# Sums of attention weights added on GpSimd, single banks of logits, and output transposes one step later

## The chip, the cores and the metric

One core of a Trainium2 chip runs one launch of the kernel. The metric is the device time of that launch in microseconds (us). Names of the engines: PE is TensorE (PEld its weight loads), DVE is VectorE, ACT is ScalarE, POOL is GpSimd, SP is SyncE, which issues most of the DMAs. PSUM has eight banks of 128 x 512 float32; a "pair" is two of them.

## The reference

The network has four layers, each an attention-like block and a feed-forward block, added to x (4 x 512 x 512, float32) with gates. The kernel runs them as stages 0 to 7 (`s0` to `s7` in the names). Two stages matter here: stage 0, cross-attention of 16 heads of 32 with 496 keys and 16 more keys of their own projection ("DCA"), and stage 6, cross-attention of 32 heads of 16 with 512 keys.

```python
def _L0_xattn_ref(x, y, Wq, bq, Wk, bk, Wv, bv, Wkv_dca, bkv_dca, ...):
    y_dca = y[:, -DCA:, :]
    y_main = y[:, :-DCA, :]
    kv_dca = (y_dca @ Wkv_dca + bkv_dca).reshape(b, DCA, 2, H, HD)
    k_dca = _ln(kv_dca[:, :, 0], kn_dca_w, kn_dca_b)
    v_dca = kv_dca[:, :, 1]
    q = _ln((x @ Wq + bq).reshape(b, s1, H, HD), qn_w, qn_b)
    ...
    k = _ln(kv[..., :HD], kn_w, kn_b)
    v = kv[..., HD:]
    ctx = _attn(qT, k, v)            # softmax over 496 keys
    ctx_dca = _attn(qT, k_dca, v_dca)
    return (ctx + DCA_WEIGHT * ctx_dca) @ Wo + bo
```

The softmax subtracts each row's maximum, takes the exponential, and divides by the sum of the weights over the keys.

## The kernel before

Products are in float32 unless bf16 is named. Stage 0 works on four batches b, in each on four groups g of four heads, in each on four tiles k of up to 128 keys, and in each tile on two pairs i of heads. One turn of the innermost loop is called a slot here: 32 slots a batch, eight a group. The logits are kept with keys on partitions and queries along the row, so that the weights can go straight into the product with the values.

A slot of stage 0 (`s0`, the loop at the end of the function) does this:

- TensorE: the logits of two heads into a pair of banks `pl` (`together`, the matmul at L262, two products on different rows of the array side by side), and, beside them, two products `ps` for the row maxima of a group to come (12 slots, `LEAD`, ahead). Then the maxima, transposed and split in three bf16 parts (`mT`), are subtracted by a product with ones into the same `pl` banks.
- ScalarE: the exponential of the pair, 128x1024, into a tile `pr` (L757). There is one `pl` buffer, so the next slot's logits wait for it.
- VectorE: the reduction of `ps` to maxima `nmx` (L634).
- TensorE: a four-head product of an earlier tile's `pr`, by the values into bank `av` in one slot of the tile, by ones into bank `sm` in the other (`weigh`; its inner `sums`, L649 and following). Both are added up over the four key tiles in PSUM.

When a group's last tile is in, `av` and `sm` are copied to `o` and `ri` on ScalarE (L671), four reciprocals of 128x128 (L673) and a product (L674) run on VectorE, then `summed` adds the DCA part: one product `pd` (L682), then `oT` (L687). After the last group of a batch, `project` multiplies by the output weights (`po`, L238), adds the bias and the residual (L772).

The next batch's projections, norms and transposes are cut into pieces (`pieces`, `todo`), and one is issued behind a slot at even distance through the first 20 slots of each batch. PSUM in stage 0 is `pl` (2 banks), two pairs `sc` that all other work shares in turn, `av` and `sm`.

The order on TensorE is partly written by hand: a product that is "tied" (`tie`, L244) follows the one tied before it; the rest is placed by the scheduler. `together` ties always, `chain` (L234) when told to.

In stage 6 a slot is alike, with three single banks of logits, two exponentials of 128x512 (L1846), a reduction per bank (L1728), and products by values in two halves of 256 queries, one half a slot. The values carry a column of ones, so the sums come with them. After a group's last half, the bank `av` is copied to `oT` on ScalarE (L1765), and `norm` (L1768) is put in the list `behind`, which is emptied one call at a slot's end: four transposes of `oT` (`s_pt`, by `flip`, L1495), a reciprocal (L1778) and a product (L1779). A piece of other work is issued at a slot's end when `behind` is empty.

Of the kernel before, what the change touches and what calls it, by code (L numbers as in the profile page):

```python
# [19 lines left out]
P = 128  # L20
# [28 lines left out]
class Net:  # L49
# [222 lines left out]
    def s0(self):  # L272
        nc, a = self.nc, self.a
        H, HD, M, ND = 16, 32, 496, 16
        LEAD = 12
        cxs = {0: self.context("s0", 0)}
        wkv = self.w("s0_wkv").rearrange("p (c n) -> p c n", c=CC)
        wq = self.w("s0_wq").rearrange("p (c n) -> p c n", c=DC)
        wd = self.u("s0_wd").rearrange("p (c n) -> p c n", c=CC)
# [16 lines left out]
        nc.sync.dma_start(wd, a["s0_wd"].rearrange("(c p) n -> p c n", p=P))  # L296
# [25 lines left out]

        def weights():
            pn = self.sc("s0_pn")[:, 0, 0:6]
            self.chain(pn, [(rep.rearrange("p r m -> p (r m)"), nw32)], tied=True)
            nc.vector.tensor_copy(nw, pn)
            nc.vector.tensor_scalar(nw[:, 0:2], nw[:, 0:2], HD**-0.5, None, op0=ALU.mult)
# [38 lines left out]
        def pieces(b):  # L366
# [11 lines left out]
            def small(k):  # L378
                room["v" + k] = self.s(f"s0_va{k}_{b}", TB * H, f"s0_va{k}")
                room[k] = self.u(f"s0_{k}4_{b}")  # L380

            def kv(k):
                if k == 0:
                    small("k")
                pkv = self.sc(f"s0_pkv_{b}_{k}")
                for i in range(2):
                    self.chain(
                        pkv[:, i, :],
                        [
                            (cx[:, c, k * P : (k + 1) * P], wkv[:, c, i * 512 : (i + 1) * 512])  # L390
                            for c in range(CC)
                        ],
                        tied=b == 0,
                    )
                dst = room["k"][:, k * 512 : (k + 1) * 512]
                nc.vector.tensor_tensor(dst, pkv[:, 0, :], bk, op=ALU.add)
                nc.scalar.copy(v4[:, k, :], pkv[:, 1, :])
# [4 lines left out]
            def half(k, y):  # L402
# [3 lines left out]
                    heads(room[k][:, y * 1024 : (y + 1) * 1024]),  # L406
# [3 lines left out]
            def turned(k, y, dst, wi):  # L410

                pt = self.sc(f"s0_pt{k}_{b}_{y}").rearrange("p i (g n) -> p i g n", g=4)
                for i in range(2):
                    for g in range(4):
                        lo = (2 * y + i) * 512 + g * P
                        nc.tensor.transpose(pt[:, i, g, :], room[k][:, lo : lo + P], self.ident)
                for i in range(2):
                    lo = (2 * y + i) * P
                    nc.scalar.activation(
                        dst[:, :, lo : lo + P], pt[:, i], AF.Identity,  # L420
                        scale=nw[:, wi : wi + 1], bias=nw[:, wi + 1 : wi + 2],
                    )

            def xT(y):
                if y == 0:
# [8 lines left out]
                    room["xT"] = self.u(f"s0_xT_{b}").rearrange("p (c n) -> p c n", c=DC)  # L434
                pt = self.sc(f"s0_ptx_{b}_{y}")
                for i in range(2):
                    for t in range(TB):
                        nc.tensor.transpose(
                            pt[:, i, t * P : (t + 1) * P],
                            room["xl"][t][:, (2 * y + i) * P : (2 * y + i + 1) * P],  # L440
                            self.ident,
                        )
                self.evict(y, room["xT"][:, 2 * y : 2 * y + 2, :], pt)

            def query(y):
                if y == 0:
                    small("q")
                pq = self.sc(f"s0_pq_{b}_{y}")
                for i in range(2):
# [3 lines left out]
                        [(room["xT"][:, c, t * P : (t + 1) * P], wq[:, c, :]) for c in range(DC)],  # L453
                    )
                nc.vector.tensor_tensor(
                    room["q"][:, y * 1024 : (y + 1) * 1024].rearrange("p (i n) -> p i n", i=2),
# [3 lines left out]
                )  # L460
                for t in (2 * y, 2 * y + 1):
                    squares(
                        f"s0q_{b}_{t}",
                        room["q"][:, t * 512 : (t + 1) * 512],
# [4 lines left out]
            def short():  # L469

                kbd = made["kbd"]
                ps = self.sc(f"s0_ld_{b}").rearrange("p i (t n) -> p (i t) n", n=256)
                for t in range(TB):
                    for g in range(4):
                        nc.tensor.matmul(
                            ps[:, t, 64 * g : 64 * (g + 1)],
                            lhsT=qT[:, g, t * P : (t + 1) * P],
                            rhs=kbd[:, b, g, :],
                            start=True, stop=True,
# [4 lines left out]
                w = self.up.tile([P, TB * H, ND], F32, tag="pr", name=f"s0_ws_{b}", bufs=4)  # L484
                nc.vector.tensor_reduce(mx, v, axis=AX.X, op=ALU.max, negate=True)
                nc.vector.tensor_tensor(w, v, wide(mx), op=ALU.add)
# [6 lines left out]
            def shortT():  # L493
                pt = self.sc(f"s0_ptw_{b}")
                for y in range(2):
                    for t in range(TB):
                        nc.tensor.transpose(
                            pt[:, y, t * P : (t + 1) * P], room["w"][:, t, y, :], self.ident
                        )
                nc.scalar.copy(wT, pt)  # L500
# [20 lines left out]
        def second():  # L521


            centre("wd", wd[:, :, 0:512].rearrange("p c (h d) -> p c h d", d=HD))
            centre("bd", heads(bd))
            pk = self.sc("s0_pkd")[0:NK, 0, :]
            self.chain(
                pk, [(cd[:, c].rearrange("p b k -> p (b k)"), wd[:, c, 0:512]) for c in range(CC)]
# [3 lines left out]
            nc.vector.tensor_tensor(kd, pk, bd[0:NK], op=ALU.add)  # L532
# [4 lines left out]
        def keys():  # L537
            kd = made["kd"]
            pt = self.sc("s0_ptd")[:, 0, 0 : 4 * NK].rearrange("p (g b k) -> p b g k", g=4, b=NB)
            for g in range(4):  # L540
                nc.tensor.transpose(
                    pt[:, :, g, :].rearrange("p b k -> p b k"),
                    kd[:, g * P : (g + 1) * P],
                    self.ident[0:NK, 0:NK],
                )
            kbd = fixed("s0_kbd", [P, NB, 4, 64])
            nc.gpsimd.memset(kbd, 0.0)
            for j in range(4):
                rows = slice(32 * j, 32 * (j + 1))
                nc.vector.tensor_scalar(  # L550
                    kbd[rows, :, :, ND * j : ND * (j + 1)], pt[rows],
                    nw[rows, 4:5], nw[rows, 5:6], op0=ALU.mult, op1=ALU.add,
                )
            cr = self.u("s0_cr")[:, 0 : CC * NB * P].rearrange(
                "p (c b r k) -> p c b r k", c=CC, b=NB, r=8
            )
# [11 lines left out]
            made["kbd"], made["cr"], made["mask"] = kbd, cr, mask  # L568
            made["vbd"] = fixed("s0_vbd", [P, NB, D])
            nc.vector.tensor_tensor(bvs[:, 0, :], bvs[:, 0, :], bvs[:, 1, :], op=ALU.add)  # L570

        def values(b):
            pv = self.sc(f"s0_pvd_{b}")[:, 0, :]
# [3 lines left out]
                    (made["cr"][:, c, b].rearrange("p r k -> p (r k)"), wd[:, c, 512:1024])  # L577
                    for c in range(CC)
                ],
            )  # L580
            nc.vector.tensor_tensor(made["vbd"][:, b, :], pv, made["mask"], op=ALU.mult)

        maxT, lead = {}, []

        def maxima():

            freed = lead

            def turn(b, g, nmx):
# [6 lines left out]
                pt = self.ps2.tile([P, TB * P], BF16, tag="sc", name=f"s0_ptm_{b}_{g}")  # L596
                for t in range(TB):
                    nc.tensor.transpose(
                        pt[:, t * P : (t + 1) * P],
                        m3[:, t].rearrange("p j k -> p (j k)"),  # L600
                        self.ident16,
                    )
                maxT[b, g] = self.vp.tile([P, S], BF16, tag="mT", name=f"s0_mT_{b}_{g}", bufs=3)
                self.evict(g, maxT[b, g], pt)

            waiting = None
            for b in range(NB):
                kT, qT = made[b][0:2]
                for g in range(4):
                    nmx = self.s(f"s0_nmx_{b}_{g}", 16, "s0_nmx")  # L610
                    for t in range(TB):
                        for y in range(2):
# [4 lines left out]
                            name = f"ps_s0_{b}_{g}_{t}_{y}"  # L617
                            if alone[0] and y:
                                ps = self.ps4.tile([P, 2, S], F32, tag="pl", name=name)
                            else:  # L620
                                ps = self.sc(name)
                            parts = []
                            for i in range(2):
                                rows = slice(32 * (2 * y + i), 32 * (2 * y + i + 1))
                                parts.append((
                                    ps[:, i, 0:M],
# [5 lines left out]
                            def after(ps=ps, nmx=nmx, at=4 * t + 2 * y):  # L632
                                with self.tc.high_priority():
                                    i = nc.vector.tensor_reduce(  # L634
                                        nmx[:, at : at + 2], ps[:, :, 0:M],
                                        axis=AX.X, op=ALU.max, negate=True,
                                    )
                                freed.append(i.ins)

                            yield parts, freed[-2:-1], after  # L640
# [3 lines left out]
        behind, later = Behind(), Behind()  # L644
        av, sm, oTs = {}, {}, {}

        def weigh(b, g, k, prs):

            v4 = made[b][2]  # L649
            n = min(P, M - k * P)  # L650
            if k == 0:
                av[g] = self.ps1.tile([P, S], F32, tag="av", name=f"s0_av_{b}_{g}", bufs=1)
                sm[g] = self.ps1.tile([P, S], F32, tag="sm", name=f"s0_sm_{b}_{g}", bufs=1)
            flags = dict(start=(k == 0), stop=(k == TB - 1))

            def part(out, lhs):
                parts = []
                for j in range(4):
                    h = slice((4 * g + j) * HD, (4 * g + j + 1) * HD)
                    parts.append((  # L660
                        out[HD * j : HD * (j + 1), :], lhs(h), prs[j // 2][0:n, j % 2, :], flags
                    ))
                self.together(parts)

            def sums():
                part(sm[g], lambda h: self.ones[0:n, 0:HD])
                if k == TB - 1:

                    o, ri = self.t(f"s0_o_{b}_{g}"), self.t(f"s0_ri_{b}_{g}")
                    nc.scalar.copy(o, av[g])  # L670
                    nc.scalar.copy(ri, sm[g])  # L671
                    for c in range(0, S, P):
                        nc.vector.reciprocal(ri[:, c : c + P], ri[:, c : c + P])  # L673
                    nc.vector.tensor_tensor(ri, ri, o, op=ALU.mult)  # L674
                    behind(summed, b, g, ri, more=True)

            part(av[g], lambda h: v4[0:n, k, h])
            later(sums, more=True)

        def summed(b, g, r):  # L680
            pd = self.sc(f"s0_pd_{b}_{g}")[:, 0, :]
            nc.tensor.matmul(  # L682
# [1373 lines left out]
```

## Time and profile before

| | us |
|---|---|
| median of 3 runs | 3339.56 |
| lowest, highest | 3332.45, 3341.3 |
| profiled execution | 3345.06 |
| its span | 3343.2 |
| mean granted TensorE clock | 0.923 of full |

| engine | busy, us | share of the span |
|---|---|---|
| PE | 2877.5 | 86% |
| PEld | 1440.6 | 43% |
| DVE | 1972.4 | 59% |
| ACT | 1215.7 | 36% |
| POOL | 629.3 | 19% |

The page of the profile gives the busy time of each engine, the span cut in 40 equal slices with the busy share of each in tenths, the chain of work that ended last, and the costliest groups of instructions, each with its line, its tiles, its count, busy time and mean duration, and what ended the idle time before it. Further views of the same trace give a table of stretches of time, the waits of one engine (who waited for whom, in total, how often, the longest), one tile's or one line's instructions, and the instructions in order of time. A line in these views may be that of a helper: all of `together` is L262, all of `chain` L238. The trace has 1.9 us outside its span.

### The profile page before, as it was taken

The page shows a single profiled execution, that of the slowest core. Times are in us where ns is not written, and L with a number is a line of the kernel's source. Part 1 is how long each engine was busy: PE and PEld are TensorE (multiplying, and loading weights), DVE is VectorE, ACT ScalarE, POOL GpSimd, SP SyncE. Part 2 cuts the span into 40 slices and gives each one's busy share as a digit, 9 for nine tenths or more (in the row PEclk, how much of TensorE's full clock was granted, in tenths as well). Part 3 has the DMA queues.
Part 4 walks back from the last instruction along what each step waited for, and adds up shares of the span by engine and source line. Part 5 has one row for each costly group of instructions (what it writes and reads, how often), then busy time and mean ns, then how long its engine had stood idle before and what let it go on. Part 6 is the DMA issues. An engine that isn't in the chain of part 4 may idle for free.

```text
span 3343.2 us, 42023 instructions
## 1 busy us (share of the span) xinstructions
PE 2877.5 (86%) x15644; PEld 1440.6 (43%) x15648; DVE 1972.4 (59%) x3148; ACT 1215.7 (36%) x1948; POOL 629.3 (19%) x509
## 2 busy tenths in 40 slices
PE   7999889959888989998845699978899999889994
PEld 3333233224444444444423588852333333254673
DVE  7555556468898979875678311138666666634103
ACT  2343433355554444432322111113544444520231
POOL 0000000006564655750000122210000000000351
PEclk8989999969899989999977699988999999989997
DMA  4000000058676777861222599972000000022798
GB/s 127 7 1 7 1 1 9 1 210 232 188 231 181 228 205 223 242 181 57 80 74 74 181 323 323 324 268 69 14 27 14 27 1 1 1 76 79 260 384 315
DMA packets 266617, 438.67 MB, mean 131 GB/s; under 512 B 32384, under 2 KB 114560, under 8 KB 264880
## 3 DMA queue, kind: packets, MB, share of 16 engines
q1 hardware_dynamic: 250352, 386.72, 36.5%
q0 software_dynamic: 13760, 45.10, 3.7%
q10 hardware_dynamic: 2304, 4.20, 0.3%
q8 instruction: 124, 2.03, 0.3%
q14 instruction: 77, 0.63, 0.1%
HBM read 370.79 MB, written 65.13 MB: 130 GB/s over the span
## 4 chain that ended last, share of the span: by engine, by line
PE 37%; DVE 7%; ACT 4%; issue 3%; POOL 2%; DMA 2%; POOLq 0%; DVEq 0%; ACTq 0%
PE s_po L238 8%; PE s_pl L262 8%; PE pg_s L238 6%; ACT pr_s L1846 3%; PE s_ph L238 2%; PE s_pq L238 2%; PE s_av L262 1%; DVE x L772 1%; DMA s_y<-s_ys 1%; PE s_pr L238 1%; PE s_pkv L238 1%; PE pt_s L217 1%; POOL s_ys L1364 1%; PE s_pb L238 1%; DVE st_s L174 1%
## 5 line engine op out<-in xcount | busy, mean ns | idle before, releaser
L1055 POOL TENSOR_TENSOR s_h<-s_h,s_C 128x512 f32<-128x512 f32 x256 | 447.6, 1749 | 302.8 <-DVE s_h L1054 264.4
L1846 ACT ACTIVATE pr_s<-s_pl 128x512 f32<-128x512 f32 x512 | 277.9, 595 | 339.2 <-PE s_ps L262 324.9
L1728 DVE TENSOR_REDUCE s_top<-s_ps 128x1 f32<-128x512 f32 x512 | 328.5, 685 | 110.6 <-PE s_ps L262 110.4
L1054 DVE TENSOR_TENSOR_SCAN s_h<-s_da,s_db 128x512 f32<-128x512 f32 x256 | 312.0, 1219 | 66.9 <-PE s_y L262 39.7
L262 PE MATMUL s_pl<-s_qT,s_kT 32*128 32x512 f32 x1024 | 293.5, 649 | 29.2 <-ACT pr_s L1846 5.7
L1053 ACT ACTIVATE s_da<-s_rdl,s_A 128x512 f32<-128x512 f32 x256 | 184.4, 722 | 336.6 <-DVE s_h L1054 334.5
L262 PE MATMUL s_ps<-s_kT,s_qT 32*128 32x512 f32 x1024 | 291.4, 661 | 7.8 <-DVE s_top L1728 5.8
L238 PE MATMUL s_ph<-xT_s,s_wu 128*128 128x256 f32 x1024 | 251.9, 402 | 0.7 <-ACT xT_s L161 0.7
L814 PE MATMUL s_acc<-s_wd,s_hT 128*128 128x512 f32 x512 | 239.9, 612 | 7.0 <-ACT s_hT L845 7.0
L262 PE MATMUL s_av<-pr_s,s_v 128*32 128x256 f32 (+2 forms) x2560 | 237.8, 443 | 0.2
L238 PEld LDWEIGHTS s_ph<-xT_s,s_wu 128*128 128x128 f32 x1024 | 200.9, 201 | 79.5 <-issue 48.2
L238 PEld LDWEIGHTS pg_s<-s_xbT,s_w 128*128 128x128 f32 (+1 forms) x1872 | 214.2, 184 | 19.8 <-issue 17.8
L634 DVE TENSOR_REDUCE s_nmx<-ps_s 128x2 f32<-128x992 f32 x128 | 151.2, 1184 | 117.3 <-PE ps_s L262 117.3
L238 PE MATMUL pg_s<-s_xbT,s_w 128*128 128x128 f32 (+1 forms) x1872 | 215.8, 276 | 1.4 <-ACT s_xbT L161 1.4
L1052 DVE TENSOR_TENSOR s_db<-s_B,s_rdu 128x512 f32<-128x512 f32 x256 | 202.7, 792 | 13.6 <-DMA s_B<-s_bc 5.9
L757 ACT ACTIVATE pr_s<-pl_s 128x1024 f32<-128x1024 f32 (+1 forms) x128 | 131.0, 1024 | 194.0 <-PE pl_s L262 164.8
L262 PE MATMUL s_y<-s_h,ident 64*64 64x512 f32 x1024 | 148.5, 643 | 52.1 <-issue 33.4
L1443 DVE TENSOR_TENSOR g_s<-g_s,pg_s 128x256 f32<-128x256 f32 x78 | 27.5, 353 | 263.7 <-ACT g_s L1442 263.7
L262 PE MATMUL pl_s<-s_qT,s_kT 32*128 32x512 f32 (+1 forms) x512 | 154.2, 680 | 26.1 <-ACT pr_s L757 23.0
L262 PE MATMUL ps_s<-s_kT,s_qT 32*128 32x496 f32 x512 | 153.5, 713 | 8.7 <-DVE s_nmx L634 7.5
L814 PEld LDWEIGHTS s_acc<-s_wd,s_hT 128*128 128x128 f32 x512 | 93.4, 192 | 152.1 <-issue 115.9
L1337 POOL DMA_INDIRECT s_xb<-s_xs,s_from x86 | 83.2, 967 | 379.8 <-PE ptr_s_xb L228 228.8
(375 smaller groups left out, 4282.7 us busy)
## 6 DMA issues: line engine op xcount, KB each, us to landing
s_B<-s_bc SPq DMA_DIRECT2D x256, 256.0 KB
s_C<-s_bc SPq DMA_DIRECT2D x256, 256.0 KB
s_w<-in_s_wg SPq DMA_DIRECT2D x39, 704.0 KB
s_w<-in_s_wu SPq DMA_DIRECT2D x39, 704.0 KB
s_w_rt<-in_s_ru SPq DMA_DIRECT2D x47, 512.0 KB
s_w_rt<-in_s_rd SPq DMA_DIRECT2D x47, 512.0 KB
s_w<-in_s_wd SPq DMA_DIRECT2D x39, 512.0 KB
s_y<-s_ys SPq DMA_DIRECT2D x32, 512.0 KB
```

What stands on the lines that cost most here:

```text
L238: ins = self.nc.tensor.matmul(out, lhsT=l, rhs=r, start=(i == 0), stop=(i == len(pairs) - 1)).ins
L262: ins = self.nc.tensor.matmul(out, lhsT=l, rhs=r, **flags).ins
L634: i = nc.vector.tensor_reduce(nmx[:, at : at + 2], ps[:, :, 0:M], axis=AX.X, op=ALU.max, negate=True,)
L757: nc.scalar.activation(prs[i][0:n], pl[0:n], AF.Exp)
L814: ins = nc.tensor.matmul(accs[i][t], lhsT=hT[:, j, t * P : (t + 1) * P], rhs=wd[f // 4][:, f % 4, :], start=(f == 0), stop=(f == FC - 1),).ins
L1052: nc.vector.tensor_tensor(db, br, du, op=ALU.mult)
L1053: nc.scalar.activation(da, dl, AF.Exp, scale=am[:, e, n : n + 1])
L1054: nc.vector.tensor_tensor_scan(h, da, db, 0.0, op0=ALU.mult, op1=ALU.add)
L1055: nc.gpsimd.tensor_tensor(h, h, cr, op=ALU.mult)
L1337: self.nc.gpsimd.indirect_dma_start(out=t, out_offset=None, in_=self.sorted[name][1], in_offset=bass.IndirectOffsetOnAxis(ap=fr[:, j : j + ...
L1728: ins = nc.vector.tensor_reduce(dst[:, i], ps[i][0], axis=AX.X, op=ALU.max, negate=True).ins
L1846: ins = nc.scalar.activation(prs[i][:, j, :], pl[j][0], AF.Exp).ins
```

## The change

In stage 0:

- The weights are added up over the four key tiles on GpSimd: for each pair of heads of a group, three additions of 128x1024, the first into a tile `es` of its own (`added`). One four-head product by ones a group then takes the place of four (`sums`), one slot after the last product by values. The bank `sm` is gone; the product goes to a pair of `sc`, as do `pd`, `po` and all other work, through one function (`dealt`).
- The product by values is made in two halves of 256 queries, one half in each of two slots.
- The logits have three single banks instead of one pair, with two exponentials of 128x512 instead of one of 128x1024. The products of a slot wait for the readers of the banks that they need (`before`).
- All products and transposes of the main loop are tied, in the order of the program. The two halves of `project` are a slot apart (`soon`), and the remaining pieces of two kinds are mixed.
- Evictions of `mT`, and of `xT` from the second batch on, are all on ScalarE. The tiles of 2048 columns are parted in two of 1024, `s0_wd` in two tiles with a DMA each, and the spread DCA keys `kbd` are made for each batch by four small copies on GpSimd. In the lead, half of the maxima's reductions are one bank each.

In stage 6 an empty entry is put into `behind` ahead of `norm`, so that the transposes come a step later.

```diff
-        wd = self.u("s0_wd").rearrange("p (c n) -> p c n", c=CC)
+        wds = [
+            self.up.tile([P, CC, 512], F32, tag="pr", name="s0_wd0", bufs=PR),
+            ut("s0_wd1").rearrange("p (c n) -> p c n", c=CC),
+        ]
...
+        sets = {"sc": 2, "pl": 3}
+        readers = {tag: [] for tag in sets}
+
+        def dealt(name, tag="sc"):
+
+            if tag == "sc":
+                t = self.sc(f"s0_{name}")
+            else:
+                t = self.ps4.tile([P, S], F32, tag=tag, name=f"s0_{name}")
+            readers[tag].append([])
+            return t, readers[tag][-1].append
+
+        def before(tag, n):
+
+            old = readers[tag][-n - sets[tag] - 1 : -sets[tag]]
+            return [r[-1] for r in old if r]
...
+        def spread(b):
+            for j in range(4):
+                rows = slice(32 * j, 32 * (j + 1))
+                nc.gpsimd.tensor_copy(
+                    kbd[b % 2][rows, :, ND * j : ND * (j + 1)], made["kc"][rows, b]
+                )
...
-                self.evict(g, maxT[b, g], pt)
+                maxT[b, g] = self.vp.tile([P, S], BF16, tag="mT", name=f"s0_mT_{b}_{g}", bufs=2)
+                read(nc.scalar.copy(maxT[b, g], pt).ins)
...
-        def weigh(b, g, k, prs):
+        def weigh(b, g, k, prs, half):
...
+            cols = slice(half * (S // 2), (half + 1) * (S // 2))
...
+                    prs[j // 2][0:n, j % 2, cols],
...
+                o = self.t(f"s0_o_{b}_{g}")
+                nc.scalar.copy(o, av[g])
+                soon(1, sums, b, g, o)
+
+        def added(b, g, k, i, pr):
+
+            n = min(P, M - k * P)
             if k == 0:
+                es[i] = pr
+                return
+            to = es[i]
+            if k == 1:
+                to = self.up.tile([P, 2, S], F32, tag="es", name=f"es_s0_{b}_{g}_{i}", bufs=ES)
+            nc.gpsimd.tensor_tensor(to[0:n], es[i][0:n], pr[0:n], op=ALU.add)
+            es[i] = to
...
-            def sums():
-                part(sm[g], lambda h: self.ones[0:n, 0:HD])
-                if k == TB - 1:
...
-            part(av[g], lambda h: v4[0:n, k, h])
-            later(sums, more=True)
+        def sums(b, g, o):
+
+            sm, read = dealt(f"sm_{b}_{g}")
+            sm = sm[:, 0, :]
+            self.together([
+                (
+                    sm[HD * j : HD * (j + 1), :], self.ones[:, 0:HD],
+                    es[b, g, j // 2][:, j % 2, :], dict(start=True, stop=True),
+                )
+                for j in range(4)
+            ])
+            ri = self.t(f"s0_ri_{b}_{g}")
+            read(nc.scalar.copy(ri, sm).ins)
+            for c in range(0, S, P):
+                nc.vector.reciprocal(ri[:, c : c + P], ri[:, c : c + P])
+            nc.vector.tensor_tensor(ri, ri, o, op=ALU.mult)
+            soon(2, summed, b, g, ri)
...
-                    behind(project, b, y, more=True)
+                    soon(2 + y, project, b, y)
...
-                        pl = self.ps4.tile([P, 2, S], F32, tag="pl", name=f"pl_s0_{b}_{g}_{k}_{i}")
+                        pl = [dealt(f"pl_{b}_{g}_{k}_{i}_{j}", "pl") for j in range(2)]
...
-                        nc.scalar.activation(prs[i][0:n], pl[0:n], AF.Exp)
+                        for j in range(2):
+                            ins = nc.scalar.activation(prs[i][0:n, j, :], pl[j][0][0:n, :], AF.Exp).ins
+                            pl[j][1](ins)
                         if after:
                             after()
-                        flush((later, behind)[i])
-                        if i == 1:
-                            behind(weigh, b, g, k, prs, more=True)
+                        added(b, g, k, i, prs[i])
+                        if i == 0:
+                            for half in range(2):
+                                soon(1 + half, weigh, b, g, k, prs, half)
+                        flush()
...
@@ stage 6 @@
                 nc.scalar.copy(oT, avs[g])
+
+                behind(lambda: None, more=True)
                 behind(norm, b, g, oT, more=True)
...
-        gp=1, cp=1, wp=3, kq=2, vp=2, up=3, bp=3, tp=6, sp=2, ps4=1, ps2=2, ps1=1
+        gp=1, cp=1, wp=3, kq=2, vp=2, up=5, bp=3, tp=5, sp=2, ps4=3, ps2=2, ps1=1
```

## The prediction

> **What bounds the kernel now.** Stage 0 takes the first 692 us and stage 6 runs from 2255 to 2958 (read from the windows of the trace); nothing else is touched. I read the page's slices first.
>
> ```profile
> PE   7999889959888989998845699978899999889994
> ...
> POOL 0000000006564655750000122210000000000351
> ...
> PEclk8989999969899989999977699988999999989997
> ```
>
> A slice is 83.6 us, so stage 0 is the first eight digits and stage 6 the 28th to 35th. In both TensorE is at 8 or 9 tenths after the first slice; in stage 0 GpSimd is idle and the granted clock 0.8 to 0.9 or so. So TensorE's own work and short waits set the time. The groups of stage 0 and their counts, by shape (window 77 to 692):
>
> ```profile
> L634 DVE TENSOR_REDUCE s_nmx<-ps_s 128x2 f32<-128x992 f32 x117 | 138.5, 1184 | 112.2 <-PE ps_s L262 112.2
> ...
> L757 ACT ACTIVATE pr_s<-pl_s 128x1024 f32<-128x1024 f32 x96 | 98.3, 1024 | 149.4 <-PE pl_s L262 126.2 <-PE ps_s L262 22.4 <-PE s_sm L262 0.5
> ...
> L673 DVE RECIPROCAL s_ri<-s_ri 128x128 f32<-128x128 f32 x64 | 54.2, 909 | 39.1 <-ACT s_ri L671 38.8
> ```
>
> The timeline then shows one slot of stage 0 (start, duration, engine, what; a block of products overlaps itself):
>
> ```profile
> 391.42 0.70 PE L262 MATMUL pl_s<-s_qT,s_kT 32*128 32x512 f32 x2 [0.17 <-ACT pr_s L757]
> ...
> 392.38 0.38 PE L262 MATMUL pl_s<-s_mT,s_ones 32*128 32x512 bf16 x2
> ...
> 392.86 1.02 ACT L757 ACTIVATE pr_s<-pl_s 128x1024 f32<-128x1024 f32 x1 [1.50 <-PE pl_s L262]
> 393.94 0.19 PEld L262 LDWEIGHTS pl_s<-s_qT,s_kT 32*128 32x128 f32 x2 [1.09 <-ACT pr_s L757]
> ...
> 395.21 1.06 PE L262 MATMUL s_sm<-pr_s,ones 128*32 128x512 f32 x8
> ...
> 396.21 0.40 PE L598 MATMUL s_ptm<-ident,s_split 128*128 128x128 bf16 x4
> ```
>
> A plain slot lasts 393.94 - 391.42 = 2.52 us: logits and maxima 0.96, the subtraction of the maxima 0.31, one block by values or by ones 1.00 (395.21 to 396.21), and a wait of about 0.2 for the exponential, which holds the only pair of logits banks. All such waits in 77 to 692 sum to 23.0 us in 41 times. A group of four heads is eight slots. In stage 6 TensorE's waits (total, times, longest) are led by one:
>
> ```profile
> PE s_pt L1495 <- ACT s_oT L1765: 30.4, 29, 1.1
> ```
>
> The output transposes stand right behind the last product by values and wait for the copy of its bank.
>
> **Sum products.** 64 blocks by ones become 16: 48 x 1.00 = **48 us** of TensorE work gone. That is the gain only where TensorE is the limit.
>
> **Plain slots.** Afterwards a slot has 0.96 + 0.31 + half a block by values. Half of 1.00 plus 0.05 gives 1.82. But the exponential begins 1.38 to 1.44 after the slot's first logits, the first half frees a bank after 0.595 (the 128x512 exponential of stage 6, L1846), and the next logits follow 0.06 later: 1.38 + 0.595 + 0.06 = 2.04. The exponential, not TensorE, then limits such a slot: gain 0.48, not 0.70. Two halves cost ScalarE 1.19 instead of 1.02, inside 2.04.
>
> **Groups with nothing beside them.** Before, the first reciprocals (L673) of such neighbours stand 22.36 us apart (545.06 to 567.42, and 603.57 to 625.93). VectorE's work per group: eight reductions x 1.19, four reciprocals 3.4, the product 0.67, the output 0.75, splits about 1.1, in all 15.4. The reciprocals are one burst, and a product that needs a bank pair waits behind it. I followed the new order slot by slot from the one that holds the sum product, at 0: sum product 1.82 to 2.85, copy to 3.5, reciprocals to 7.0, the waiting reduction to 8.2. The pair products of the DCA values (`pd`) are now dealt into the same rotation of two pairs and are tied, so they wait from 6.2 to 8.2; the next maxima wait another 1.35 behind the product. Six other slots take 2.04, and the next sum product's slot begins at 21.8. Gain **0.57 a group**: the burst takes back nearly all of 8 x 0.48 - 1.00.
>
> **Groups with pieces of the next batch beside them.** TensorE is full there. In 20 of 32 slots a batch, 0.50 goes and 1.00 per group comes back: 20 x 0.50 - 2.5 = 7.5. The remaining twelve give between nothing and 0.47 each; with the rows above I take 8 to 9.7 a batch, together some **38 us** in stage 0. Batch 3's last twelve slots have no maxima and keep 0.45 each; they are in that sum.
>
> **GpSimd's additions.** Six of 128x1024 a group. The nearest row is stage 4's addition of half the size (its source's durations, ns: least 1265, median 1772, most 3504; 128x512, two operands in SBUF, VectorE busy beside it). Doubled: 2.53 to 7.0 us, and 3.5 by the mean of 1749. I take 2.5 to 3.5, since stage 0's VectorE mostly reads PSUM while stage 4's multiplies and scans SBUF tiles all the time. In the order above the sum product wants the last addition at 23.6; the additions become ready at 2.6, 5.4, 7.5, 13.8, 16.2 and 18.2. At 2.53 the last ends at 21.3, hidden; at 3.5 at 24.3, 0.6 late. From 3.3 on they show, and at 5 the group is GpSimd's, 30 us.
>
> The row also says that the two engines disturb each other: the stage 4 product on VectorE (L1052) has a least time of 686, a mean of 792 and a most of 1771 ns. The product behind the reciprocals (L674) reads two SBUF tiles while additions run; a wait of up to one addition there delays a reduction and so TensorE. I charge 3 to 8 us for stage 0.
>
> [...]
>
> **Other edits of stage 0.** The sums after the last group wait for the last addition and their copy: +2 us, at the end, uncovered. In the lead, six pair reductions become twice as many single-bank ones, about +1. The eight-product output block (L238, `po`) is parted and moved one slot; eleven evictions move from VectorE (L162, 0.42 for the maxima) to ScalarE; an exponential may wait behind one, 0 to 5 us in all: I take 0, since most fall in slots where TensorE is full. The waits behind table loads (up to 3.9 us of `pl` on ScalarE, some four places) stay. SP: the loads for the next stages wait now for the last group's addition and weights, still ahead of the last output, so ctx, which comes last, is not later; if that cover failed, their issue (506 to 514 us before) costs up to 8.
>
> **Clock.** In 10-us windows of stage 0 the granted clock falls to 0.50 to 0.76 where TensorE waited some 2 us or more; over the stretches at 0.87 to 0.94 the missing share of the clock times their length comes to some 44 us of stage 0. New waits of 2.05 and 1.35 us close together could bring more such windows (2 to 3.5 us each), and fewer waits elsewhere fewer: ±10, taken as 0.
>
> Stage 0: -38 + 2 + 1 + (3 to 8, say 3) = **-32 us**.
>
> **Stage 6.** A slot with the transposes lasts 3.36 (2420.39 to 2423.75), its neighbours 1.81 (2427.43 to 2429.23).
>
> ```profile
> 2422.52 0.59 ACT L1765 COPY s_oT<-s_av 128x512 f32<-128x512 f32 x1
> ...
> 2423.16 0.66 PE L1495 MATMUL s_pt<-ident,s_oT 128*128 128x128 f32 x4 [1.06 <-ACT s_oT L1765]
> ```
>
> One step later the four transposes still cost 0.60, but by then the copy, which ends 2.7 to 2.95 after that slot's start, is done before TensorE reaches them, at 3.6 or later. The 1.06 goes. What is late next is the exponential chain: 5.7 us in 28 times already, of which a part may go too. The queue behind the transposes is the next slot's logits, as before; reciprocal and product come a slot later on VectorE, which is 1.29 busy in 1.81 and has room for 0.68. Bounds 25 to 35; I take the row, 30.4, and 1 more: **-31**.
>
> **Sum.** -32 - 31 = -63 against the profiled execution: 3345.1 (span 3343.2) to 3282. That execution lies 5.5 above the median of the runs, 3339.6; from there the forecast is **3276**.
>
> **Rivals.**
> 1. *All of the sum products' time comes out* (0.17): the burst is hidden, the exponential chain shortens with the pairs gone, half of the 23.0 of waits go. -48 - 11, stage 6 -33: 3340 - 92 = 3248. For it: TensorE 8 to 9 tenths busy. Against: 2.04 by the exponential's row.
> 2. *Only one stage gives* (0.20): stage 0's gain is eaten by the burst, the additions' disturbance of VectorE and a colder clock, stage 6 keeps its 31: 3309; or the reverse, the exponential takes the place of the copy in stage 6 and stage 0 keeps 32: 3308. For it: 0.57 a group against 48 us of work removed.
> 3. *GpSimd becomes the bound and the kernel is slower* (0.08): at 5.3 us an addition a group takes 32 us of GpSimd, and the sum product waits for it. The eight intervals between first reciprocals that were 20.3 to 33.6 before (210 in sum) and some 1.8 less after are stretched to 32: 256 - 210 + 14 = 60 lost, the point from which there is no gain. At 6 us, 36 a group, it is 32 more and 2 of the next interval: 94, so 3276 + 94 = 3370. For it: the 3504 row, doubled. Against: the median, doubled, is 3.5.
> 4. *Little moves* (0.05): the ties and the additions at about 5 us just balance stage 6: 3335.
>
> The forecast has 0.50. The range 3243 to 3318 takes in the first two rivals and leaves out the last two, 0.13. Faster by over 0.3% (10 us, about what a measurement here can tell from none): 0.50 + 0.17 + 0.20 = 0.87; within 0.05; slower 0.08.
>
> **What would show it.** In the profile after: first reciprocals of bare groups 21 to 22.5 us apart; plain slots of about 2.04; additions of 128x1024 between 2.5 and 3.5 us; `pd` waiting for VectorE some 2 us in bare groups; the wait for L1765 gone and stage 6 some 31 us shorter; stage 0 ending at about 660. Additions of over 4 us, or a wait of the sum product for GpSimd in most groups, would make it wrong.

## The result and the profile after

| | before | after |
|---|---|---|
| median of the runs, us | 3341.16 (12 runs) | 3342.31 (12 runs) |
| span of the profiled execution, us | 3343.2 | 3344.0 |
| stage 0, to the next stage's first product (`s_pi`), us | 691.1 | 722.4 |
| TensorE idle in stage 0, from 80 us on, us | 59.1 | 113.9 |
| time lost to a lower granted clock there, us | 43.8 | 74.0 |
| stage 6, first input transpose to last output product, us | 710.7 | 681.3 |

The ratio of after to before is 1.0003, 95% interval 0.9993 to 1.0013: no change that can be measured, where 63 us less were forecast. The two stages went opposite ways: stage 6 gave 29 us and stage 0 took 31. The fourth row is the sum over stretches of 4 us of the time in which TensorE is not busy, the fifth that of their length times the missing share of the clock; where TensorE waits at a low clock both count it, 5.4 us of before and 7.9 of after. What is left of stage 0 from 80 us on, about TensorE's work at full clock, went from 509 to 456 us. So the 48 us of sum products did go, with 3 to 5 more; 55 us of waiting and 30 us of low clock came in their place.

The rows of the page of after that were shown of before:

```profile
PE   6888887877998998998855699995999999989994
...
POOL 0333334424565554770000022210000000000351
...
PEclk8889998778998998999976699996999999989997
```

GpSimd is busy for some three tenths of the first eight slices; TensorE has lost about a tenth there, and in the eighth slice the clock has fallen to 7. TensorE's waits in the first 720 us (total, times, longest):

```profile
PE s_pl L262 <- ACT pr_s L859: 28.9, 30, 4.2
PE s_pd L238 <- DVE s_nmx L693: 20.7, 10, 3.2
PE s_pl L262 <- DVE s_nmx L693: 16.7, 7, 4.0
...
PE s_sm L262 <- POOL es_s L750: 2.0, 1, 2.0
```

The sum product waits for GpSimd once, at the end. The waits that grew are for VectorE's reductions (L693; L634 before), since before these were:

```profile
PE ps_s L262 <- DVE s_nmx L634: 7.5, 9, 1.4
...
PE s_pd L682 <- DVE s_nmx L634: 1.8, 2, 0.9
...
PE pl_s L262 <- DVE s_nmx L634: 0.8, 1, 0.8
```

In stage 6 the wait for the copy is gone (of 30.4 before):

```profile
PE s_pt L1599 <- ACT s_oT L1869: 0.7, 1, 0.7
```

Why VectorE is late shows in the durations of its instructions that have both operands in SBUF, the on-chip memory beside PSUM, or cast one from there (least, median, most in ns; line by line, before first: the casts and the differences that split the maxima, and the product behind the reciprocals):

```profile
L593 DVE CAST s_split<-s_nmx x48: 190/203/205, 70.1 to 633.9; 128x16 bf16<-128x16 f32 x48
...
L595 DVE TENSOR_TENSOR s_nmx<-s_nmx,s_split x32: 111/185/189, 70.4 to 633.6; 128x16 f32<-128x16 f32 x32
...
L674 DVE TENSOR_TENSOR s_ri<-s_ri,s_o x16: 674/676/692, 139.1 to 674.8; 128x512 f32<-128x512 f32 x16
```

```profile
L647 DVE CAST s_split<-s_nmx x48: 135/203/2355, 75.9 to 657.1; 128x16 bf16<-128x16 f32 x48
...
L649 DVE TENSOR_TENSOR s_nmx<-s_nmx,s_split x32: 183/185/2327, 76.1 to 656.9; 128x16 f32<-128x16 f32 x32
...
L750 POOL TENSOR_TENSOR es_s<-es_s,pr_s x64: 2337/2347/3172, 103.2 to 697.8; 128x1024 f32<-128x1024 f32 x32, 112x1024 f32<-112x1024 f32 x32
...
L770 DVE TENSOR_TENSOR s_ri<-s_ri,s_o x16: 675/1400/2626, 143.0 to 705.8; 128x512 f32<-128x512 f32 x16
```

The medians of casts and differences are as before, but their most is the length of one addition (15 of the 80 lasted longer than before, counted in the trace); the product's median itself has doubled. One group's burst in the timeline of after:

```profile
587.58 2.34 POOL L750 TENSOR_TENSOR es_s<-es_s,pr_s 128x1024 f32<-128x1024 f32 x1 [1.26 <-ACT pr_s L859]
587.69 2.29 DVE L647 CAST s_split<-s_nmx 128x16 bf16<-128x16 f32 x1
589.87 1.18 DVE L693 TENSOR_REDUCE s_nmx<-s_ps 128x2 f32<-128x992 f32 x1
590.97 0.73 DVE L780 SCALAR_TENSOR_TENSOR s_oT<-s_pd,s_bvs,s_ri 128x512 f32<-128x512 f32 x1
...
591.19 1.22 PE L262 MATMUL s_pl<-s_qT,s_kT 32*128 32x512 f32 x2 [4.03 <-DVE s_nmx L693]
```

A cast of 128x16, 0.2 us of work, starts 0.11 after an addition and ends when the addition does (at 589.98; 587.58 + 2.34 = 589.92). The reduction queued behind it ends 2.1 us late. The logits are issued together with the product for the next maxima, which needs that reduction; they wait 4.03, of which the cast made 2.1. When TensorE goes on it is slow: the pair takes 1.22 instead of 0.70.

### The profile page after: what moved, and what is told of

It is laid out like the page before. It is cut to its first block, busy times and chain, and to the rows that moved or that the text cites. A ratio compares the mean times of both kernels' runs of the same rounds, so it can differ in the third digit from the quotient of the medians.

```text
span 3344.0 us, 42659 instructions
## 1 busy us (share of the span) xinstructions
PE 2854.8 (85%) x15772; PEld 1448.2 (43%) x15776; DVE 2000.9 (60%) x3140; ACT 1229.3 (37%) x2087; POOL 859.4 (26%) x622
## 4 chain that ended last, share of the span: by engine, by line
PE 37%; DVE 7%; ACT 3%; issue 3%; DMA 2%; POOL 2%; SPq 0%; POOLq 0%; DVEq 0%; ACTq 0%
PE s_po L238 8%; PE s_pl L262 8%; PE pg_s L238 6%; ACT pr_s L1952 2%; PE s_ph L238 2%; PE s_pq L238 2%; PE s_av L262 2%; DMA s_y<-s_ys 1%; DVE x L876 1%; PE s_pkv L238 1%; PE s_pr L238 1%; PE pt_s L217 1%; POOL s_ys L1468 1%; PE s_pb L238 1%; POOL s_xb L1441 1%
## 5 line engine op out<-in xcount | busy, mean ns | idle before, releaser
L262 PE MATMUL s_pl<-s_qT,s_kT 32*128 32x512 f32 (+1 forms) x1536 | 462.4, 679 | 78.8 <-ACT pr_s L859 28.9
L262 PE MATMUL s_ps<-s_kT,s_qT 32*128 32x512 f32 (+1 forms) x1536 | 450.7, 689 | 13.9 <-DVE s_top L1832 5.9
L262 PE MATMUL s_av<-pr_s,s_v 128*32 128x256 f32 (+1 forms) x3072 | 258.9, 410 | 0.2
L262 PEld LDWEIGHTS s_pl<-s_qT,s_kT 32*128 32x128 f32 (+1 forms) x1536 | 121.9, 192 | 248.8 <-ACT pr_s L1952 95.9
L859 ACT ACTIVATE pr_s<-s_pl 128x512 f32<-128x512 f32 (+1 forms) x256 | 138.8, 595 | 200.4 <-PE s_pl L262 167.9
L693 DVE TENSOR_REDUCE s_nmx<-s_ps 128x2 f32<-128x992 f32 x122 | 144.4, 1184 | 94.2 <-PE s_ps L262 94.2
L750 POOL TENSOR_TENSOR es_s<-es_s,pr_s 128x1024 f32<-128x1024 f32 (+1 forms) x64 | 152.9, 2395 | 170.6 <-ACT pr_s L859 170.2
L262 PEld LDWEIGHTS s_av<-pr_s,s_v 128*32 128x32 f32 (+1 forms) x3072 | 62.2, 110 | 297.6 <-issue 265.5
```

Source lines behind the costliest of these rows:

```text
L262: ins = self.nc.tensor.matmul(out, lhsT=l, rhs=r, **flags).ins
L693: ins = nc.vector.tensor_reduce(nmx[:, at : at + 2], pair[:, :, 0:M], axis=AX.X, op=ALU.max, negate=True,).ins
L750: nc.gpsimd.tensor_tensor(to[0:n], es[i][0:n], pr[0:n], op=ALU.add)
L859: ins = nc.scalar.activation(prs[i][0:n, j, :], pl[j][0][0:n, :], AF.Exp).ins
```

## The experiments

Theory A: the additions delay VectorE, instruction by instruction, and through the reductions behind them TensorE. Theory B: the burst of reciprocals and the tied order stop TensorE by themselves. Ratios below are to runs of the kernel before on the same chip, with 95% intervals; times are medians.

**Stage 6 alone.** The kernel before with one line more.

```diff
                 nc.scalar.copy(oT, avs[g])
+                behind(lambda: None, more=True)
                 behind(norm, b, g, oT, more=True)
```

> The kernel before with the stage 6 edit alone. The forecast's term for stage 6 says 31 us less than before, about 3309. Rival: stage 6 became shorter in the changed kernel only because its start was moved by stage 0; then this run equals the kernel before, about 3340.

Measured: 3307.1 against 3339.12, 0.9904 (0.9887 to 0.9920). Stage 6 is 31 us shorter (2236.5 to 2915.8 against 2247.0 to 2957.7). The term of stage 6 holds by itself.

**No additions.** The function `added` does nothing, and the sum product reads ones.

```diff
-                    es[b, g, j // 2][:, j % 2, :], dict(start=True, stop=True),
+                    one, dict(start=True, stop=True),
```

> The changed kernel without GpSimd's additions: the sum product reads a constant tile of ones, so the sums of the weights are left out. All products stay. Theory A, the additions delay VectorE: the product behind the reciprocals goes back from 1.55 to 0.68 us and the casts and differences of the maxima from 0.5 to 0.2, 39 us of VectorE in all, most of it with TensorE waiting and then running at a lower clock: 3282 to 3302. Theory B, the burst of reciprocals and the tied order stop TensorE by themselves: those durations shrink, but the waits of pd and of the logits for the maxima stay, 3322 to 3342.

Measured: 3281.2, 0.9833 (0.9813 to 0.9852): 0.8 below theory A's range, far from theory B's. Stage 0 ends at 663.7; from 80 to 660 TensorE is idle for 83.9 us and loses 39.1 to the clock. Casts, differences and product are back at 200, 184 and 684 ns in the mean. The wait of `pd` stays, smaller:

```profile
PE s_pl L262 <- ACT pr_s L851: 28.7, 30, 4.2
PE s_pd L238 <- DVE s_nmx L693: 14.7, 10, 1.9
```

So the burst is real, but the additions cost 1.0003 - 0.9833 = 1.7%, 57 us, with some 0.2% of uncertainty.

**Additions that only write.** In the program each is replaced by two fills of nearly 128x1024 and two copies of one column of each head.

```diff
-            nc.gpsimd.tensor_tensor(to[0:n], es[i][0:n], pr[0:n], op=ALU.add)
+            nc.gpsimd.tensor_copy(to[0:n, :, 0:1], pr[0:n, :, 0:1])
+            nc.gpsimd.memset(to[0:n, :, 1:S], 1.0)
+            nc.gpsimd.memset(to[0:n, :, 1:S], 1.0)
+            nc.gpsimd.tensor_copy(to[0:n, :, 0:1], pr[0:n, :, 0:1])
```

> The changed kernel with each addition replaced by GpSimd work of about the same length that writes the same tile but reads only one column of the weights, before and after two fills (the sums are left out). GpSimd stays as busy, the exponentials and the sum product wait for it as before. If VectorE is delayed because GpSimd reads its operands (theory A), the time is that of the run without additions, within 10 us. If the chain through GpSimd (buffers of weights, the tile of sums) is what costs, it is that of the changed kernel, about 3342.

Measured: 3352.32, 1.0037 (1.0023 to 1.0052), slower than the changed kernel. Neither expectation was met, and the time can't be set beside them, since the fills did not keep the additions' places: they need only the tile, so the twelve of a group ran nearly in a row, for some 11 us, as soon as the sum product had read it (482.7 to 493.6 in one group). What the run shows is in its durations (casts, differences, product):

```profile
L647 DVE CAST s_split<-s_nmx x48: 131/758/4319, 75.2 to 677.6; 128x16 bf16<-128x16 f32 x48
...
L649 DVE TENSOR_TENSOR s_nmx<-s_nmx,s_split x32: 178/185/189, 75.4 to 677.3; 128x16 f32<-128x16 f32 x32
...
L773 DVE TENSOR_TENSOR s_ri<-s_ri,s_o x16: 671/678/693, 137.8 to 719.1; 128x512 f32<-128x512 f32 x16
```

What reads two tiles in SBUF is free again; the casts, which read one, wait longer than ever, over several fills:

```profile
196.21 1.83 POOL L751 MEMSET es_s<- 112x1022 f32 x2
...
196.46 3.42 DVE L647 CAST s_split<-s_nmx 128x16 bf16<-128x16 f32 x1
196.54 3.34 DVE L693 TENSOR_REDUCE s_nmx<-s_ps 128x2 f32<-128x992 f32 x1
...
197.99 1.84 POOL L752 MEMSET es_s<- 112x1022 f32 x2
```

The reduction behind the cast ends with it (199.88). There are two kinds of collision in these runs. One is with an instruction of two SBUF operands, only when GpSimd reads much: differences lasted up to 2327 ns and the product up to 2626 beside the additions, and 189 and 693 here. The other is with a cast, also when GpSimd writes: up to 2355 beside the additions and up to 4319 beside the fills, which take 947 in the mean, so over four of them. What in the two engines makes them wait was not shown.

**No reciprocals.** The four of a group are left out, and with them the division.

```diff
-            for c in range(0, S, P):
-                nc.vector.reciprocal(ri[:, c : c + P], ri[:, c : c + P])
```

> The changed kernel without the four reciprocals a group (the division by the sums is left out). 54 us of VectorE go, in bursts of 3.4. Theory B, the burst is what stops TensorE: the waits of pd (20.7) and of logits for maxima (16.7) nearly go, with some of the low clock, 3282 to 3302. Theory A: the additions still delay the product and the splits; 3320 to 3335.

Measured: 3313.89, 0.9916 (0.9899 to 0.9933), between the two. The wait of `pd` falls from 20.7 to 2.8, but that of the logits for a reduction rises from 16.7 to 32.8: without the reciprocals casts and differences fall on additions more often (means of 704 and 899 ns). Taking out 54 us of VectorE's work gives half of what taking the additions out gives, some 29 us.

**Splits on GpSimd.** Casts and differences move to GpSimd, a slot earlier in its order.

```diff
-                    nc.vector.tensor_copy(m3[:, :, :, i], v)
+                    nc.gpsimd.tensor_copy(m3[:, :, :, i], v)
                     if i < 2:
-                        nc.vector.tensor_tensor(v, v, m3[:, :, :, i], op=ALU.subtract)
+                        nc.gpsimd.tensor_tensor(v, v, m3[:, :, :, i], op=ALU.subtract)
...
+                            if waiting and t == 0 and y == 1:
+                                parted(*waiting)
```

> The changed kernel with the three casts and two differences that split the maxima on GpSimd, a slot earlier in its order. On VectorE they took 24.7 us more than before, waiting for additions, and the reductions queued behind them. If these waits are the larger part of the loss: 3302 to 3317. If the product behind the reciprocals alone matters, or GpSimd's own queue delays the maxima as much: about 3342.

Measured: 3288.2, 0.9831 (0.9812 to 0.9850): better than expected, as good as no additions at all, though the product still waits (mean 1119 ns).

```profile
L647 POOL CAST s_split<-s_nmx x48: 250/254/1147, 72.4 to 611.8; 128x16 bf16<-128x16 f32 x48
...
L649 POOL TENSOR_TENSOR s_nmx<-s_nmx,s_split x32: 221/230/234, 72.7 to 611.5; 128x16 f32<-128x16 f32 x32
```

On GpSimd they queue behind additions too (in one group an addition of 2.35 us starts at 549.18, and the next cast at 551.47), but the transposes that need them waited no longer (6.5 us in all, 7.4 in the changed kernel), and no reduction stands behind them. The logits' wait for a reduction fell from 16.7 to 0.4; that of `pd` stayed, longer than the 14.7 without additions:

```profile
PE s_pd L238 <- DVE s_nmx L698: 20.7, 10, 3.2
```

So the product's waits do reach TensorE, with about 6 us of waiting (20.7 - 14.7). They are made up for elsewhere: the splits' own 16 us have left VectorE as well, and the logits' wait is below the 6.9 of the run without additions. No run has the splits on GpSimd without additions, so how much of the gain is this relief stays open; at the rate of the run without reciprocals (29 us for 54) it would be some 8, an estimate. Stage 0 ends at 667.5, with 88.0 idle and 37.4 lost to the clock (80 to 664). This kernel is faster than both.

**Splits early, on VectorE.** The control: the same earlier place, `nc.vector` kept.

> The changed kernel with the splits still on VectorE but a slot earlier in the program, as in the run that moved them to GpSimd (3288). If the engine is what mattered there, VectorE still waits for additions and the time stays between 3325 and 3350. If the earlier place was what mattered: below 3300.

Measured: 3338.99, 1.0004 (0.9993 to 1.0015). The place alone does nothing; the engine is what mattered.

**Casts alone, on ScalarE.**

```diff
-                    nc.vector.tensor_copy(m3[:, :, :, i], v)
+                    nc.scalar.copy(m3[:, :, :, i], v)
```

> The changed kernel with only the three casts of the splits on ScalarE, the two differences still on VectorE. Of the 24.7 us that the splits wait in it, 14 are in casts and 10.7 in differences. If casts and differences cost alike: about half of the gain of the run with all five on GpSimd, 3305 to 3320. If either alone stops VectorE as long, since one addition is waited for in any case: 3325 or more.

Measured: 3309.61, 0.9916 (0.9897 to 0.9935), half of the 1.7%. The differences still wait (mean 451 ns). Casts and differences cost about alike.

**Product on GpSimd.** The product moves to GpSimd, one slot later, and `pd` two.

```diff
-            nc.vector.tensor_tensor(ri, ri, o, op=ALU.mult)
-            soon(2, summed, b, g, ri)
+            soon(1, times, ri, o)
+            soon(4, summed, b, g, ri)
+
+        def times(ri, o):
+            nc.gpsimd.tensor_tensor(ri, ri, o, op=ALU.mult)
```

> The changed kernel with the product behind the reciprocals on GpSimd, a slot later, and the DCA product two slots later than now. VectorE loses 24.7 us, 13.9 of them waiting, and pd no longer falls into the burst of reciprocals. Theory A (VectorE's waits for additions): 3317 to 3327, the splits still wait. Theory B (burst and tied order): below 3310, since pd's 20.7 us of waits go.

Measured: 3361.56, 1.0044 (1.0027 to 1.0061), against both theories as put. The additions that stand behind the product on GpSimd now start later, and the splits, still on VectorE, meet them more (total and mean behind the bar):

```profile
L649 DVE TENSOR_TENSOR s_nmx<-s_nmx,s_split 128x16 f32<-128x16 f32 x32 | 47.4, 1480 | 1.0
L647 DVE CAST s_split<-s_nmx 128x16 bf16<-128x16 f32 x48 | 38.9, 810 | 1.6
```

That is 86 us instead of 40 in the changed kernel. That the shifted additions are the reason was only read from the trace.

**Both moves.**

> Both of these moves. Then nothing of a group's chain on VectorE has two operands in SBUF or is such a cast, and the time should come near the run without additions (3281): 3283 to 3300. Rival: GpSimd's queue, now additions, product and splits in one order, becomes what the exponentials or the transposes of the maxima wait for: over 3310.

Measured: 3292.05, 0.9831 (0.9804 to 0.9857), the same ratio as the splits alone. The wait of `pd` is gone, but TensorE now waits 21.4 us for splits (`s_ptm`), which share GpSimd's queue with the product. So this run does not give the price of the product's waits.

**Additions in halves.**

```diff
-            nc.gpsimd.tensor_tensor(to[0:n], es[i][0:n], pr[0:n], op=ALU.add)
+            for j in range(2):
+                nc.gpsimd.tensor_tensor(to[0:n, j], es[i][0:n, j], pr[0:n, j], op=ALU.add)
```

> The changed kernel with each addition in two halves of 128x512. If VectorE's instruction waits for the end of the addition that is running and then goes first, its waits halve: 3310 to 3325. If it waits until GpSimd has nothing to run, or the halves cost more in sum, no gain: 3340 or more.

Measured: 3334.12, 0.9973 (0.9958 to 0.9987), a gain of 0.3%, short of the 3310 to 3325. The longest wait halves:

```profile
L647 DVE CAST s_split<-s_nmx x48: 137/203/1272, 74.6 to 660.2; 128x16 bf16<-128x16 f32 x48
```

So VectorE waited for the half that ran (1282 to 1323 ns in the mean, by shape), not for an idle GpSimd. But the sum of the splits' waits does not fall (means of 552 and 562 ns, from 490 and 513): 29 of the 80 instructions now meet a half, where 15 met a whole addition.

**Splits on GpSimd and `pd` two slots later.**

```diff
-            soon(2, summed, b, g, ri)
+            soon(4, summed, b, g, ri)
```

> Splits on GpSimd, and the DCA product two slots later, behind the burst of reciprocals instead of in it. The 20.7 us that pd waits there go; if nothing takes their place 3268 to 3278, if the next maxima's product waits behind the same burst instead, 3284 to 3294.

Measured: 3285.71, 0.9839 (0.9811 to 0.9866), no gain over the splits alone. `pd` no longer waits for a reduction, but the logits that start with the next maxima do: 18.3 us in 12 times, for the same burst. That rival holds.

## Why the prediction was wrong

- **Stage 6**: right. 31 us were forecast; 29 came in the changed kernel and 31 with the edit alone.
- **Sum products, single banks and the burst of reciprocals**: right in mechanism and nearly in size. TensorE's work fell by 50 to 53 us. Without the additions the first reciprocals of bare groups stand 21.73 us apart (492.59 to 514.32; 21.8 was worked out), and stage 0 ends at 663.7 where some 657 followed (692 - 35). Plain slots take 2.01 and 2.08 in the changed kernel (logits at 641.67, 643.68 and 645.76), where 2.04 was worked out. The whole is 3281 where the forecast said 3276.
- **GpSimd's additions**: their length, 2.35 to 2.44 us in the mean, lay just below the 2.5 to 3.5 that was taken, and they are hidden, as forecast: the sum product waited for them once, 2.0 us, at the end.
- **The step that failed** is "I charge 3 to 8 us for stage 0" for the disturbance of VectorE. It cost 57. The working looked at the one long instruction with two SBUF operands, the product (L674), and for that one the size was right: its waits came to about 6 us of `pd`'s. What it left out are the five small instructions that split the maxima. They were listed among VectorE's work ("splits about 1.1") and not asked whom they would meet; with them on GpSimd the kernel is as fast as without additions, and in the same place on VectorE it is not faster at all. What counted was not an instruction's own length but how many there are in a group, that one which met an addition waited to its end (15 of the 80, up to 2355 ns), and that the reductions TensorE needs stand behind them in VectorE's queue.
- **Clock**: "±10, taken as 0" came to 30 us in the profiled executions. Without the additions the loss is 39.1, no more than before (43.8). But some 12 of the 30 lie in one stretch behind a wait that is there without the additions too (last section), so how much of the lower clock the delayed reductions brought is not settled.
- **Rivals**: the second named the burst, the disturbance and a colder clock for stage 0, but let them only cancel its gain, with 3309; they took 31 us more. The fourth had nearly the right time, 3335, by the wrong reason, additions of about 5 us.

Open: which waits of casts come from GpSimd's reading and which from its writing in the changed kernel, what the splits' departure from VectorE gives beside the end of their collisions, and why the lower clock, once there, held as long as it did.

## What to carry to other kernels

Before work is given to GpSimd, list every VectorE instruction that runs beside it, the smallest first, and what stands behind each in VectorE's queue: here a cast of 0.2 us that lasted 2.29 beside an addition made the reduction behind it 2.1 late, and so TensorE. When such a collision is found, try the small instructions on the engine that holds the long ones, where nothing urgent stands behind them; here that turned no change into 1.7%. And test a change of two places apart: one line in stage 6 was worth 31 us and could not be seen beside stage 0.

## What the runs showed of the hardware

In the changed kernel two kinds of VectorE instruction waited for a running addition (2347 ns in the median) to its end: those with two operands in SBUF (a difference up to 2327 ns, the product up to 2626), and the casts (up to 2355). When GpSimd only filled and copied single columns, differences and product kept their length (185 and 682 in the mean), and the casts waited longer (up to 4319 beside fills of 947). Two more rows were longer there: the norm's `s_xl`, with one SBUF tile (2120 in the mean, 525 in the changed kernel), and `s_oT` (1683, where the changed kernel has at most 751); whether these waited themselves or behind a cast stays open. Reductions from PSUM kept their length beside additions (1184 ns in the mean before and after); beside the fills they took 1362 in the mean, and the one shown above, queued behind a waiting cast, 3.34 us and ended with it. Halving GpSimd's additions halved the longest wait of a cast (1272 ns, from 2355) and left the splits' sum (means of 552 and 562, from 490 and 513).

The lower clock held for a long time in which TensorE did not pause. In these rows of the changed kernel (stretch, length, then busy time and count of PE, PEld, DVE, ACT, POOL, then the granted clock, the DMA share and GB/s) it is at half speed for two whole rows, with PE busy throughout:

```profile
650.00:660.00 10.00, 5.03 (x36) 1.57 (x28) 6.10 (x12) 2.56 (x5) 4.65 (x2) 0.73 0.00 0
660.00:670.00 10.00, 10.00 (x40) 2.44 (x38) 0.75 (x1) 2.79 (x6) 4.69 (x2) 0.50 0.00 0
670.00:680.00 10.00, 10.00 (x46) 2.59 (x42) 0.00 (x0) 3.00 (x6) 4.68 (x2) 0.50 0.01 2
680.00:690.00 10.00, 9.89 (x56) 2.65 (x52) 3.67 (x5) 5.06 (x10) 4.25 (x2) 0.74 0.00 0
```

One wait of 5 us, for a split behind the burst, was followed by a loss of about 15 us ((1 - 0.73 + 0.50 + 0.50 + 1 - 0.74) x 10). Without the additions the same wait (4.95 us) was followed by one of 3.4:

```profile
600.00:610.00 10.00, 4.98 (x48) 1.74 (x48) 7.55 (x13) 3.74 (x8) 0.00 (x0) 0.93 0.00 0
610.00:620.00 10.00, 9.72 (x49) 2.75 (x48) 0.75 (x1) 3.73 (x7) 0.00 (x0) 0.73 0.00 0
```

With additions both occur: the profile of the splits on GpSimd has no long stretch here (0.85, 0.81 and 1.00 from 605 to 635), the one with `pd` two slots later has one (0.70, 0.50, 0.50 and 0.77 from 600 to 640). So the wait alone did not decide how long the low clock held.
